# Loading image halves on two queues, constants behind the first image, weights prepared on GpSimd

## Chip, core and metric

The kernel runs on one core of a Trainium2 chip. The metric is the device time of one execution in microseconds. The engines are TensorE (PE; its weight loads are shown as PEld), VectorE (DVE), ScalarE (ACT), GpSimd (POOL) and SyncE (SP). SP and ACT each issue DMAs on a queue of their own.

## What is computed

The input `x` holds 2 batches ("images" below) of 56 channels of 128 by 128 numbers in float32. Two layers of a Fourier neural operator with attention are applied, each with a residual. `_conv_ref` is the same function for both, with its own weights:

```python
def fno_layer(x, w, b, sw, sb, norm=False, act=False):
    y = spectral_conv(x, w, b)          # rfft2, 32x16 modes times weights, irfft2
    if norm: y = inorm(y)
    y = y + skip1x1(x, sw, sb)
    return gelu(y) if act else y

def _conv_ref(x, ...):
    xa = x.reshape(B * K, 1, H, W)
    xn = inorm(xa, g1, b1)
    k, q, v = (fno_layer(xn, ...) for each of K, Q, V)      # 8 heads
    attn = softmax(einsum(q, k) / sqrt(H * W))              # over the 56 channels
    out = fno_layer(einsum(attn, v), Pw, Pb, Psw, Psb)
    att = inorm(out + xa, gan, ban)
    an = inorm(att, g2, b2)
    h = fno_layer(an, M0..., norm=True, act=True)
    h = fno_layer(h, M1..., norm=True, act=False)
    return inorm(h, gmo, bmo) + att

x = x + _conv_ref(_gn(x), layer 0 weights)    # _gn: group norm, 32 groups
x = x + _conv_ref(_gn(x), layer 1 weights)
```

## The kernel before

The Fourier transforms are matrix products with constant matrices. All constants lie in one array `const["all"]`; its first 128 columns are the identity, which the transposes need, and the rest (`group`, `fw`, `raw`, `same` and others) go into the tile `C` as well. `stage` takes the spectral weights of a layer, `smt` (tiles `sm0`, `sm1`) the small parameters of the two layers, each row spread over 128 partitions.

`X2` holds both images. An image is loaded as 8 DMAs of 448 KB (L209): for each pair `g` of row groups, one for each row half `c`, which goes to partitions 0 to 55 or 64 to 119. Two further DMAs (L214) fill the rows between.

The work of an image runs through stages:

- `turn` calls `turned` for 8 tiles. For each, PE transposes 16 pieces (L363) into a PSUM tile `pair`, of which there are three; ACT copies it to the plane `P` (L368); DVE takes two statistics (L373).
- `modes_chain` aggregates the statistics (L458), averages over groups on PE (L462), takes the square root on ACT (L466), scales the plane on DVE (L479) and ACT (L477), and transforms it (L483, L488, L386). POOL puts the factors into columns of `P` (L491, L493), PE turns them (L501), ACT copies the result to `gvr` (L503).
- `gram` sums the Gram matrix of the channels in 128 matmuls (L511), followed by `gram_chain`. `scale_x` multiplies `X2` by `gvr` on DVE (L550).
- `scores` (L597, L578), `softmax_chain` (L637 on), `values` (L620), `mix_chain`, `heads`, `norms_chain`, `gelu`, `h_chain` and `end` follow.

The weights go a way of their own. `prepare(layer, first, second)` combines weights and constants in elementwise operations (L255 to L302): those named `first` on one engine, those named `second` on another. Four wide ones (L270 to L273) come first, then two `product`s (L294 to L302), and `place` (L284 to L289) writes the result into `stage`. `relay` transposes that (L320, L324, L331) into `tc` (L335), and POOL widens `tc` into `WU` (`build`, L341), later into `WT` and `WM`. POOL also prepares parts of the scores (L572).

The two images are woven together by hand: the stages are generators that yield estimates of their cost, and `_woven` puts the second one's pieces between those of the first. A scheduler of the framework then orders the instructions of each engine by its own estimates, so an engine's final order isn't that of the source. It also puts in the semaphores. DMAs of both queues share eight of them in turn, so the issue of a DMA waits until the one eight places before it has landed.

Of the kernel before, what the change touches and what calls it, by code (L numbers as in the profile page):

```python
# [42 lines left out]
B, K, N = 2, 56, 128  # L43
# [11 lines left out]
N_CONST = sum(n for _, n in _PARTS.values())  # L55
# [73 lines left out]
N_SMALL = sum(n for _, n in _COLS.values())  # L129
# [11 lines left out]
def _woven(lead, *bulks):  # L141

    rest = chain(*bulks)
    for want in lead:
        while want > 0:
            cost = next(rest, None)
            if cost is None:
                break
            yield cost
            want -= cost  # L150
    yield from rest
# [9 lines left out]
def _run(units):  # L161
    for _ in units:
        pass
# [3 lines left out]
def fno_layers(ctx: ExitStack, tc: tile.TileContext, x, out, weights, small, const):  # L167
    nc = tc.nc
    V, S, G, T = nc.vector, nc.scalar, nc.gpsimd, nc.tensor
# [24 lines left out]
    Ct = cp.tile([N, N_CONST], F32, name="C")  # L194
# [1 line left out]
    ident = C["ident"]  # L196
    nc.scalar.dma_start(out=ident, in_=const["all"][:, :N])
    stage = cp.tile([N, 1632], F32, name="stage")
    nc.scalar.dma_start(out=stage[:, :1088], in_=weights[0].rearrange("p m r n t -> p (m r n t)"))
    smt = [cp.tile([N, N_SMALL], F32, name=f"sm{n}") for n in range(2)]  # L200
    for n in range(2):
        nc.scalar.dma_start(out=smt[n], in_=small[n : n + 1, :].to_broadcast([N, N_SMALL]))
    nc.scalar.dma_start(out=Ct[:, N:], in_=const["all"][:, N:N_CONST])
    X2 = xp.tile([N, B, 64, N], F32, name="X2")
    xin = x.rearrange("b k (g c r) w -> c b k g (r w)", c=2, r=8)
    for b in range(B):
        for g in range(0, 8, 2):
            for c in range(2):
                nc.sync.dma_start(  # L209
                    out=X2[64 * c : 64 * c + K, b, 8 * g : 8 * g + 16, :].rearrange("p (g r) w -> p g (r w)", r=8),  # L210
                    in_=xin[c, b, :, g : g + 2, :],
                )
    for b in range(B):
        nc.sync.dma_start(out=X2[K:64, b], in_=x[b, :8, :64, :])  # L214
    eps = cp.tile([N, 1], F32, name="eps")
# [138 lines left out]
    def turned(b, g, L, stats):  # L354
        p = pair()
        for s in range(2):
            for e in range(4):
                i = 8 * g + 4 * s + e
                if L == 0:
                    for c in range(2):  # L360
                        q = slice(64 * c, 64 * c + K)
                        o = K * (4 * s + e)
                        T.transpose(p[:, c, o : o + K], X2[q, b, i, :], ident[q, q], tile_position=(64 * c, 0))  # L363
                else:
                    T.transpose(p[:, s, N * e : N * e + 120], X2[:120, b, i, :], ident[:120, :120])  # L365
        dst = P[b][:, 896 * g : 896 * g + 896]
        if L == 0:
            S.copy(dst.rearrange("p (x c k) -> p c x k", x=8, c=2), p[:, :, :448].rearrange("p c (x k) -> p c x k", x=8))  # L368
        else:
            src = p.rearrange("p s (e c k) -> p (s e) c k", e=4, c=2)  # L370
            S.copy(dst.rearrange("p (x c k) -> p x c k", x=8, c=2), src[:, :, :, :K])  # L371
        for s in range(2):
            V.bn_stats(stats[:, 2 * g + s, :], dst[:, 448 * s : 448 * s + 448])  # L373

    def turn(b, stats):
        for g in range(8):
            turned(b, g, 0, stats)
            yield 0.9
# [74 lines left out]
    def new_stats(b):  # L453
        return little(f"stats{b}", [N, 16, 6])
# [478 lines left out]
    prs = [None, None]  # L933
    st = [[{}, {}], [{}, {}]]
    stats = [new_stats(b) for b in range(B)]
    par, d, cpt, tcs = prepare(0, V, G)
    prs[0] = par, d
    _run(turn(0, stats[0]))
    _run(_woven(
        chain(modes_chain(0, 0, stats[0], st[0][0]), relay(cpt, tcs, WT[:, 2048:3072], [(0, 16)])), turn(1, stats[1]),  # L940
    ))
# [1 line left out]
    for L in range(2):  # L943
# [13 lines left out]
        if L == 0:  # L957
            nc.sync.dma_start(out=stage[:, :1088], in_=weights[1].rearrange("p m r n t -> p (m r n t)"))
            par, d, cpt, tcs = prepare(1, G, G)
# [3 lines left out]
        stats = [new_stats(b) for b in range(B)] if L == 0 else [None, None]  # L963
# [61 lines left out]
```

## Time and profile before

| | us |
|---|---|
| runs of the kernel before | 555.65, 557.22, 564.92 |
| median | 557.22 |
| span of the profiled execution | 555.1 |
| PE busy in it | 457.0 (82%) |
| DVE busy | 337.0 (61%) |
| ACT busy | 190.2 (34%) |
| POOL busy | 184.3 (33%) |

The page gives the profiled execution's own time as its span, from the first to the last instruction; the fastest of the three runs is 0.55 us longer than it. The shares are averages over all stages. How an edit at the kernel's head acts is read from the head itself: from the chain of waits, which follows the last work back to what released it, from the timelines of the engines, and from tables of busy time in short stretches. A line such as `9.78 1.76 ACT L368 COPY P<-pair ... x2 [5.16 <-PE pair L363]` gives start, length, engine, line, operation, output and input, number of instructions, and in brackets the idle time ahead of it and what ended it. `SPq` and `ACTq` are the issue of DMAs.

### The profile page before, as it was taken

What the parts mean: (1) busy time and instruction counts of PE and PEld (TensorE: products, weight loads), DVE (VectorE), ACT (ScalarE), POOL (GpSimd) and SP (SyncE); (2) the same over time, 40 slices, a digit from 0 to 9 for tenths busy, and PEclk for the clock granted to TensorE, in tenths of its full rate; (3) what the DMA queues carried; (4) which work ended last, traced back from release to release, by engine and by line L of the source; (5) the groups of instructions that cost most, each with busy time, mean ns of one, the idle gap of its engine ahead of it and who ended that gap; (6) DMA issues with size and microseconds to landing.
All of it is one profiled execution on the core that took longest, in us unless ns stands there. A gap on an engine that the chain in (4) does not pass through costs nothing.

```text
span 555.1 us, 14768 instructions
## 1 busy us (share of the span) xinstructions
PE 457.0 (82%) x6630; PEld 316.3 (57%) x6630; DVE 337.0 (61%) x577; ACT 190.2 (34%) x238; POOL 184.3 (33%) x194
## 2 busy tenths in 40 slices
PE   2447889799999999798688859989999999979390
PEld 1423858669685555455563447768967556535250
DVE  0576478932717665869459995841253865677751
ACT  2344132063437556233103314124454656602000
POOL 2460424920271000065456871630000000035566
PEclk9999689899998999988667959989999999988586
DMA  8993000050000000056144541030000000017687
GB/s 202 213 197 58 4 2 2 5 145 4 2 3 1 1 2 1 1 166 198 53 132 133 168 127 14 2 105 4 2 2 2 1 1 2 2 33 225 191 230 285
DMA packets 16303, 40.58 MB, mean 73 GB/s; under 512 B 2528, under 2 KB 3296, under 8 KB 16224
## 3 DMA queue, kind: packets, MB, share of 16 engines
q1 hardware_dynamic: 15520, 38.25, 25.5%
q10 hardware_dynamic: 720, 1.39, 1.0%
q8 instruction: 52, 0.85, 0.6%
q14 instruction: 11, 0.09, 0.1%
HBM read 24.69 MB, written 14.68 MB: 71 GB/s over the span
## 4 chain that ended last, share of the span: by engine, by line
PE 43%; DVE 26%; DMA 8%; ACT 7%; POOL 7%; issue 5%; SPq 2%; POOLq 0%; ACTq 0%; DVEq 0%
PE pair L766 5%; DVE X L550 4%; PE pair L801 4%; PE pair L751 4%; PE pair L597 4%; DVE stats L373 4%; PE bank L511 3%; PE bank L578 3%; DMA C<-const_all 3%; DMA X<-store 3%; POOL P L918 3%; PE bank L690 3%; PE bank L789 2%; PE bank L483 2%; DMA xr<-store 2%
## 5 line engine op out<-in xcount | busy, mean ns | idle before, releaser
L821 DVE BATCH_NORM_STATS2 stats<-P 128x6 f32<-128x512 f32 x64 | 40.5, 681 | 19.3 <-ACT P L819 19.2
L916 DVE SCALAR_TENSOR_TENSOR P<-P,hs,pair 128x1024 f32<-128x1024 f32 x32 | 40.0, 1269 | 18.7 <-PE pair L766 18.7
L918 POOL TENSOR_TENSOR X<-P,xr 128x1024 f32<-128x1024 f32 x16 | 39.9, 2500 | 30.5 <-DVE P L916 16.5
L550 DVE TENSOR_TENSOR X<-X,gvr 120x1024 f32<-120x1024 f32 x32 | 49.3, 1568 | 0.0
L373 DVE BATCH_NORM_STATS2 stats<-P 128x6 f32<-128x448 f32 x64 | 35.7, 610 | 20.1 <-ACT P L368 10.1
L819 ACT ACTIVATE P<-pair 128x1024 f32<-128x1024 f32 x32 | 32.6, 1026 | 32.0 <-PE pair L766 31.3
L395 POOL MEMSET WT<- 128x256 f32 x4 | 1.3, 313 | 121.0 <-PE bank L789 88.3
L766 PE MATMUL pair<-X,Be 57*64 57x512 f32 x256 | 41.1, 742 | 0.0
L511 PEld LDWEIGHTS bank<-P 128*64 128x64 f32 (+1 forms) x1024 | 37.1, 158 | 2.9 <-issue 2.6
L511 PE MATMUL bank<-P 128*64 128x56 f32 (+1 forms) x1024 | 38.7, 244 | 0.0
L801 PEld LDWEIGHTS pair<-C,P 120*128 120x128 f32 x256 | 26.8, 143 | 20.9 <-issue 12.3
L766 PE MATMUL pair<-X,Bs 57*64 57x512 f32 x256 | 37.5, 627 | 0.0
L751 PE MATMUL pair<-C,WT 32*128 32x128 f32 x512 | 26.7, 319 | 11.3 <-DVE P L916 5.5
L597 PE MATMUL pair<-xf,WU 64*64 64x56 f32 x1024 | 35.9, 220 | 0.0
L597 PEld LDWEIGHTS pair<-xf,WU 64*64 64x64 f32 x1024 | 32.8, 134 | 5.0 <-issue 3.9
L751 PEld LDWEIGHTS pair<-C,WT 32*128 32x128 f32 x512 | 21.6, 214 | 23.6 <-issue 9.1
L801 PE MATMUL pair<-C,P 120*128 120x120 f32 x256 | 34.3, 277 | 0.4 <-ACT P L819 0.2
L341 POOL TENSOR_TENSOR WT<-tc,C 128x1024 f32<-128x1024 f32 x8 | 26.5, 3341 | 20.0 <-ACT tc L335 11.9
L802 ACT COPY WT<-pair 128x896 f32<-128x896 f32 x32 | 28.8, 906 | 12.5 <-PE pair L801 12.3
L363 PE MATMUL pair<-C,X 56*128 56x56 f32 x256 | 17.5, 292 | 18.6 <-DMA X<-x 12.8
L371 ACT COPY P<-pair 128x896 f32<-128x896 f32 x16 | 14.4, 902 | 46.7 <-PE pair L365 46.7
L365 PE MATMUL pair<-C,X 120*128 120x120 f32 x128 | 20.3, 313 | 10.2 <-POOL X L918 9.2
(249 smaller groups left out, 868.8 us busy)
## 6 DMA issues: line engine op xcount, KB each, us to landing
X<-x SPq DMA_DIRECT2D x16, 448.0 KB
xr<-x SPq DMA_DIRECT2D x32, 224.0 KB
store<-X SPq DMA_DIRECT2D x32, 224.0 KB
out<-P SPq DMA_DIRECT2D x32, 224.0 KB
xr<-store SPq DMA_DIRECT2D x16, 224.0 KB
X<-store SPq DMA_DIRECT2D x16, 224.0 KB
C<-const_all ACTq DMA_DIRECT2D x1, 621.0 KB
stage<-weights ACTq DMA_DIRECT2D x1, 544.0 KB
```

The source lines that it names most:

```text
L373: V.bn_stats(stats[:, 2 * g + s, :], dst[:, 448 * s : 448 * s + 448])
L511: T.matmul(p[u : u + m, :K], lhsT=P[b][:, K * i : K * i + m], rhs=plane[b][:, i, :], start=(i < 2), stop=(i == N - 1), tile_position=(0, u ...
L550: V.tensor_tensor(v, v, _bc(st["gvr"][:120], 1, 8), ALU.mult)
L597: T.matmul(p[64 * e : 64 * e + 64, k, K * a : K * a + K], lhsT=WUv[64 * e : 64 * e + 64, t + k, a, :], rhs=xv[64 * e : 64 * e + 64, t + k, ...
L751: T.matmul(both[j // 2][:, j % 2, N * e : N * e + N], lhsT=Z[32 * j : 32 * j + 32, o : o + N], rhs=C["gw"][32 * j : 32 * j + 32, :], start ...
L766: T.matmul(p[64 * c : 64 * c + 64, r, :], lhsT=Bs[q, :], rhs=X2[q, b, s : s + 4, :].rearrange("p e w -> p (e w)"), start=False, stop=True, ...
L801: T.transpose(p[:, r, N * e : N * e + 120], h3[:120, o : o + N], ident[:120, :120])
L802: S.copy(hT[v].rearrange("p r e c k -> p (r e) c k"), p.rearrange("p r (e c k) -> p (r e) c k", e=4, c=2)[:, :, :, :K],)
L819: S.activation(h3, both[v].rearrange("p r m -> p (r m)"), AF.Gelu)
L821: V.bn_stats(stats[:, 4 * A + 2 * v + r, :], h3[:, 512 * r : 512 * r + 512])
L916: V.scalar_tensor_tensor(h3, h3, st["hs"], both[v].rearrange("p r m -> p (r m)"), ALU.mult, ALU.add)
L918: G.tensor_tensor(dst, h3, back(n), ALU.add)
```

## The change

Each image's row half 0 is loaded by SP and row half 1 by ACT; before, SP loaded both. The identity is still the first DMA of ACT. The weights of layer 0 move from ACT's queue to SP's, behind image 0's loads; the rest of the constants stays on ACT but goes behind image 0's loads; the two small parameter rows go to the end of ACT's list. `prepare(0, ...)` is called behind image 0's `turn`, and with POOL as both engines, where DVE was the first and POOL the second.

```diff
     nc.scalar.dma_start(out=ident, in_=const["all"][:, :N])
     stage = cp.tile([N, 1632], F32, name="stage")
-    nc.scalar.dma_start(out=stage[:, :1088], in_=weights[0].rearrange("p m r n t -> p (m r n t)"))
     smt = [cp.tile([N, N_SMALL], F32, name=f"sm{n}") for n in range(2)]
-    for n in range(2):
-        nc.scalar.dma_start(out=smt[n], in_=small[n : n + 1, :].to_broadcast([N, N_SMALL]))
-    nc.scalar.dma_start(out=Ct[:, N:], in_=const["all"][:, N:N_CONST])
     X2 = xp.tile([N, B, 64, N], F32, name="X2")
     xin = x.rearrange("b k (g c r) w -> c b k g (r w)", c=2, r=8)
     for b in range(B):
         for g in range(0, 8, 2):
             for c in range(2):
-                nc.sync.dma_start(
+                (nc.sync, nc.scalar)[c].dma_start(
                     out=X2[64 * c : 64 * c + K, b, 8 * g : 8 * g + 16, :].rearrange("p (g r) w -> p g (r w)", r=8),
                     in_=xin[c, b, :, g : g + 2, :],
                 )
+        if b == 0:
+            nc.scalar.dma_start(out=Ct[:, N:], in_=const["all"][:, N:N_CONST])
+            nc.sync.dma_start(out=stage[:, :1088], in_=weights[0].rearrange("p m r n t -> p (m r n t)"))
+    for n in range(2):
+        nc.scalar.dma_start(out=smt[n], in_=small[n : n + 1, :].to_broadcast([N, N_SMALL]))
...
     stats = [new_stats(b) for b in range(B)]
-    par, d, cpt, tcs = prepare(0, V, G)
+    _run(turn(0, stats[0]))
+    par, d, cpt, tcs = prepare(0, G, G)
     prs[0] = par, d
-    _run(turn(0, stats[0]))
     _run(_woven(
         chain(modes_chain(0, 0, stats[0], st[0][0]), relay(cpt, tcs, WT[:, 2048:3072], [(0, 16)])), turn(1, stats[1]),
     ))
```

## The prediction

> **What bounds the kernel now.** I read the chain of waits first, over the first 150 us, then the timelines of ScalarE (ACT) and SyncE (SP), then the table of busy time in 2 us stretches. The chain's columns are start, length, engine and line.
>
> ```profile
> 2.85 17.36 DMA C<-const_all
> 20.31 0.73 DVE stage L270
> ...
> 26.61 7.92 DVE stats L373 x15
> 34.55 0.60 DVE mv L458
> 35.48 0.60 PE bank L462 x2
> 37.41 1.23 DVE P L479
> 38.77 3.17 PE bank L483 x10
> ...
> 62.85 4.46 PE bank L511 x86
> ```
>
> The constants take until 20.3 us to land. VectorE (DVE) then prepares the weights (L270 to L289) and only afterwards works off sixteen statistics of image 0, so the mode chain of image 0 starts at 34.6, its first matmul L483 at 38.8 and its Gram matrix L511 at 62.8. From there TensorE (PE) is near full: 48.8 of the 54.7 us up to the first softmax (L637 at 117.5) are PE busy.
>
> ```profile
> 3.34 1.28 ACT L368 ACT_TABLE_LOAD   x1 [3.34 <-issue]
> 9.78 1.76 ACT L368 COPY P<-pair 128x896 f32<-128x896 f32 x2 [5.16 <-PE pair L363]
> ```
>
> ACT is free of its five DMA issues at 3.3 us and empties the first transposed tile at 9.8. SP waits inside its own list of loads:
>
> ```profile
> SPq L209 <- DMA C<-const_all: 7.4, 2, 3.8
> SPq L209 <- DMA stage<-weights: 4.5, 1, 4.5
> SPq L209 <- DMA sm<-small: 4.1, 2, 2.2
> ```
>
> A load is not issued until an older transfer, of whatever queue, has landed: there are eight semaphores for DMAs, and the ninth DMA reuses the first's. The last table tells the rate (last two columns: DMA share, GB/s):
>
> ```profile
> 4.00:6.00 2.00, 0.14 (x1) 0.14 (x2) 0.00 (x0) 0.62 (x1) 0.00 (x0) 1.00 1.04 236
> 6.00:8.00 2.00, 0.33 (x2) 0.15 (x2) 0.00 (x0) 0.00 (x0) 0.00 (x0) 1.00 1.01 263
> 20.00:22.00 2.00, 0.90 (x16) 0.90 (x18) 1.65 (x3) 0.00 (x0) 0.00 (x0) 1.00 0.92 203
> ```
>
> With large rows on both queues the DMA engines move 236 to 263 GB/s, with SP's images alone about 200.
>
> **What the Trainium skill says.** "DMA: Bandwidth & Descriptors", Issuing engines are not separate DMA queues: both queues run on the same 16 engines, and a second issuer saves only issue time. The trace agrees on the sharing (weights, 544 KB, took until 11.1 us beside images) but the stretches above show some rate gained. The same page, Anatomy of one DMA — SWDGE (gpsimd) path: a semaphore wait is held by the issuing sequencer, not by the DMA engine; SP's waits above agree. "SBUF — State Buffer", Who interferes with whom: a GpSimd (POOL) operation and a DVE operation with two SBUF inputs lock each other out; here DVE L550 takes 1.22 us alone and three take 7.71 beside POOL's L341 at 91.7. "TensorE: Matmul & The Clock Gate", What's actually happening: a PE that has idled runs at half clock for some 3.4 us; here sixteen L331 take 3.75 us at 57.3 and 1.96 at 88.2.
>
> **The change, part by part** (line numbers of the kernel before; the order is that of the program as built.) Call X1 to X16 the sixteen 448 KB loads; odd ones go to SP, even ones to ACT.
>
> *1. What is gained.* DVE loses about 5.5 us of L270 to L289, and image 0 is loaded first. Landing at 234 KB/us (240 GB/s, my choice between 203 and 263): the identity and X1 by 5.8 as before, then 896 KB in 3.8 us per pair, X8 at 20.5 instead of 25.8. A chain that started then would save some 10 us. It doesn't start then.
>
> *2. ACT's queue, the main cost.* ACT now has ten DMA issues ahead of its first copy L368 instead of five, and seven carry a wait. In order: identity, X2, X4, X6, X8 (waits for the identity), constants (X2), X10 (X4), X12 (X6), X14 (X8), X16 (constants), sm0 (X10), sm1 (X11). So ACT can empty no tile until X10 and X11 have landed. After 20.5: weights beside X8 and constants (rows over 4 KB, which got about 40% of the bytes beside images before: 544 KB in 5.3 us of 263 GB/s) are done at 22.6 and 26.8, X9 at 25.7, X11 at 29.2, X10 at 30.6. Issuing sm0 and sm1 takes 1.0 (they took 1.18), the table load 1.28: first copy F = 33 instead of 9.8. At 262 GB/s F is 31, at 205 it is 37. Behind it wait PE (three pair buffers, so PE stops after three tiles), the statistics, everything. SP's own waits delay nothing: each is met before its queue runs dry.
>
> *3. From F to the first L483.* The built order puts L462 of image 0 after half of image 1's transposes and all L483 of image 0 after the rest. From F: DVE takes 16 statistics at 0.55, from F+0.9 to F+9.7; with two of image 1 and the aggregate 0.59, L462 runs at F+11.7. ACT copies (0.88 each) keep pace. Then tiles 13 to 16 cold at 1.2 us; ACT takes the square root only after copy 14 and a table load, F+17.3; DVE with statistics between reaches L479's end at F+20. Image 1 has landed by 42, no wait. First L483 at 53 instead of 38.8.
>
> *4. From L483 to L511.* It was 24 us with image 1's transposes between; now nothing is between, but PE idles on DVE: L483 cold 2.5, then the alternation of L488 (1.0) and L479 (1.2) and four more statistics of image 1 brings L386 to +11, L386 1.7, L498 and L503 0.9, one L550 1.2 (now ahead), L324 1.4, L331 cold 3.7: +20. L511 starts at 73 instead of 62.8: 10 us late.
>
> *5. GpSimd.* L270 to L289 on POOL, priced from the same lines of layer 1 (all on POOL): the three 544-wide at 1.35, the rest 10.8, small columns of both layers 5.8, L273 0.6, L572 four at 0.56. But sm0 stands behind X16 on ACT's queue: 1344 KB after X10 at 117 KB/us is 42.1, plus 2.4 as before, 44.5. After it 19.5 us remain, then L491 and L493 1.6: 65.6. L501 needs L493's output, and step 4 has L501 at F+32.7 = 65.7. So POOL is covered, by nothing to spare; each us more would be paid in full.
>
> *6. L511 to the softmax.* Equal PE work. Before, PE idled 5.9 us there. Now L483 of image 1 comes after the whole of L511 and waits for L479, behind four L550 that share the lock with L341: DVE ready at +14, PE there at +12. L386's chain of 7 to 9 us has only 6 of PE work beside it. Three L620 now precede the last L331 and wait 1.2 for POOL. Idle sum 8 to 9; against it the fixed chains could shorten by 2. I take +2; bounds -2 and +4. The tile order is the same on every engine after the softmax, bar POOL memsets and three early xr loads, both at nothing: POOL is idle from 132 to 149 and the DMA engines are idle from 46 us. All later work follows by data, so the shift stays.
>
> *Sum.* 10 + 2 = 12 on the span of 555.1: 567. The three runs' median is 2.1 above the span (the fastest is 0.55 above), so 569.
>
> **The rivals.**
> R1, POOL is the bound: if DVE's L479 and copies lock it out, or sm0's 128 short rows share worse, L493 ends 6 us later, L511 at 79: 575. For it: one L302 of layer 1 took 0.89 us where others take 0.44, and one L284 0.65 instead of 0.32. Against: from 26 to 34 us POOL ran such lines beside DVE 93% busy.
> R2, not slower by 2%, by one mechanism: two queues hold the 262 GB/s of 6 to 10 us. Then F is 31, L511 at 71, +8; with image 1 turned before L511, its chain fills PE and step 6 gives -2: +6, 563. It decides from about 245 GB/s with step 6 at zero. For it: the two stretches shown. Against: those rows were the weights', and stretches with constants show 238 to 246.
> R3, the change does what it says: ACT is not held, tiles leave as they land. Image 1's tiles are then done at 42, L511 at 62 if POOL too were early, 556; with POOL as in step 5 it is again 73. Against it: the waits stand in ACT's list ahead of the copies.
>
> **How the numbers follow.** Forecast 569: 0.40; R1 575: 0.17; R2 563: 0.38; R3 556: 0.05. Two per cent, about what a measurement of this kernel can tell from no change, is 546 to 568. Forecast and R1 make slower 0.57; R2 and R3 make the same 0.41, faster keeps 0.02. The range is 560 to 579: rate (2 to 4 us each way), step 6 (-4 to +2), R1 to its end.
>
> **What would show it.** Right: ACT's first copy L368 near 33 us, DVE idle before; constants landed by 27 and unused; L483 near 53, L511 near 73, softmax near 129; POOL's L255 waiting for sm till 44. Wrong: a copy of image 0 before 25 us, or L511 before 66. Rate right if X10 lands near 31.

## The result, and the profile after

The changed kernel takes 574.54 us (median of four runs, 573.5 to 578.59), the kernel before 557.33 beside it (555.65 to 564.92). The ratio is 1.0327, with a 95% interval of 1.0285 to 1.037: slower by 17 us. The profiled execution's span grew from 555.1 to 572.0. In what follows the ratios and intervals leave out executions in a slower state, the medians count them, and of e15_one_queue, whose profile is of a slower execution, only the head up to 43 us is read, where TensorE's clock was full. From L205 on, a line of the changed kernel has a number one higher than before: L368 is now L369, L511 is L512.

The chain of waits over the first 150 us (start, length, what) begins quite differently from before:

```profile
1.92 11.65 DMA X<-x
13.60 14.41 DMA X<-x
28.03 17.25 DMA sm<-small
...
65.57 0.41 POOL P L494 x2
66.03 0.81 PE bank L502 x2
...
73.42 3.60 PE bank L512 x64
```

Two image loads, the second issued when the first has landed, take until 28.0; only then are the small rows issued, and they need 17 us to land. The chain then goes through GpSimd to L494, which TensorE waits for, and so to L512 at 73.4 (62.8 before). ScalarE's timeline shows the queue that holds both:

```profile
1.17 4.96 ACTq L205 DMA_DIRECT2D X<-x  x4
10.34 0.36 ACTq L210 DMA_DIRECT2D C<-const_all  x1
13.60 11.58 ACTq L205 DMA_DIRECT2D X<-x  x4
28.03 0.84 ACTq L213 DMA_DIRECT2D sm<-small  x2
28.90 1.28 ACT L369 ACT_TABLE_LOAD   x1 [28.90 <-DMA X<-x]
30.20 4.14 ACT L369 COPY P<-pair 128x896 f32<-128x896 f32 x5
```

The first copy starts at 30.2, where it was at 9.8. The four issues at 13.60 take 11.58 us because each waits for an older transfer. GpSimd's and TensorE's timelines show the second hold:

```profile
45.35 0.21 POOL L256 TENSOR_TENSOR der<-sm 128x8 f32<-128x8 f32 x1 [15.67 <-DMA sm<-small]
```

```profile
66.03 0.80 PE L502 MATMUL bank<-C,P 128*128 128x128 f32 x2 [4.19 <-POOL P L494]
```

GpSimd waits 15.67 us for the small rows, and TensorE later 4.19 for GpSimd. The table of busy time in 2 us stretches shows that the two queues do move more than the 200 GB/s of SyncE's images alone:

```profile
10.00:12.00 2.00, 1.64 (x30) 1.64 (x31) 0.00 (x0) 0.00 (x0) 0.00 (x0) 1.00 0.94 290
18.00:20.00 2.00, 0.00 (x0) 0.00 (x0) 0.00 (x0) 0.00 (x0) 0.00 (x0) 1.00 0.91 273
```

In the second stretch all five engines stand at zero: the data arrive, and nobody works on them.

How far the changed kernel is behind at a few places (start in us):

| place | before | after | shift |
|---|---|---|---|
| first copy, L369 | 9.78 | 30.20 | 20.4 |
| first L484 | 38.77 | 48.87 | 10.1 |
| first L512 | 62.78 | 73.35 | 10.6 |
| softmax of image 0, L638 | 117.50 | 129.17 | 11.7 |
| softmax of image 1, L638 | 145.33 | 159.43 | 14.1 |
| first L917, end of layer 0 | 235.26 | 248.46 | 13.2 |
| eighth L917 | 261.89 | 278.31 | 16.4 |
| first L459 of layer 1 | 283.60 | 300.05 | 16.5 |
| span | 555.1 | 572.0 | 16.9 |

Two thirds of the loss are there at the first softmax. The rest comes later, mostly in two places: between the two softmaxes, and between the first and the eighth L917. The first of them is visible in VectorE's timeline, and GpSimd's for the same stretch:

```profile
143.85 0.62 DVE L707 SCALAR_TENSOR_TENSOR P<-P,D 128x448 f32<-128x448 f32 x1
144.51 3.12 DVE L708 TENSOR_TENSOR P<-P,D 128x448 f32<-128x448 f32 x1
```

```profile
143.88 0.68 POOL L710 COPY bm<-P 1x56 f32<-1x56 f32 x1 [3.15 <-DVE P L703]
144.52 1.33 POOL L271 TENSOR_TENSOR stage<-stage,C 128x544 f32<-128x544 f32 x1
145.82 1.33 POOL L272 TENSOR_TENSOR stage<-stage,C 128x544 f32<-128x544 f32 x1
```

L708 takes 3.12 us, in step with two wide products of layer 1's preparation. In the kernel before, it took 0.62, and GpSimd came to those products only 17 us after it. A memset that waits for TensorE stood ahead of them; in the changed kernel it comes behind them, at 163.3:

```profile
132.83 0.62 DVE L707 TENSOR_TENSOR P<-P,D 128x448 f32<-128x448 f32 x1
```

```profile
149.24 0.32 POOL L395 MEMSET WT<- 128x256 f32 x1 [16.37 <-PE pair L620]
149.51 1.35 POOL L270 TENSOR_TENSOR stage<-stage,C 128x544 f32<-128x544 f32 x1
```

### The profile page after: what moved, and what is told of

Same layout as the page of the kernel before. It is cut to its first block, busy times and chain, and to the rows that moved or that the text cites. A ratio compares the mean times of both kernels' runs of the same rounds, so it can differ in the third digit from the quotient of the medians.

```text
span 572.0 us, 14762 instructions
## 1 busy us (share of the span) xinstructions
PE 459.6 (80%) x6630; PEld 320.7 (56%) x6630; DVE 334.2 (58%) x558; ACT 189.4 (33%) x238; POOL 190.1 (33%) x213
## 4 chain that ended last, share of the span: by engine, by line
PE 42%; DVE 24%; DMA 12%; POOL 7%; ACT 7%; issue 5%; SPq 1%; POOLq 0%; ACTq 0%; DVEq 0%
PE pair L767 6%; DVE X L551 5%; DMA X<-x 5%; PE pair L752 4%; PE pair L802 4%; PE pair L598 4%; PE bank L579 3%; PE bank L691 3%; DMA sm<-small 3%; DMA X<-store 3%; PE bank L512 3%; DVE P L917 3%; PE bank L790 2%; PE bank L442 2%; PE bank L387 2%
## 5 line engine op out<-in xcount | busy, mean ns | idle before, releaser
L374 DVE BATCH_NORM_STATS2 stats<-P 128x6 f32<-128x448 f32 x64 | 35.9, 608 | 41.5 <-ACT P L369 30.0
L551 DVE TENSOR_TENSOR X<-X,gvr 120x1024 f32<-120x1024 f32 x32 | 51.7, 1642 | 4.5 <-ACT gvr L504 4.5
L917 DVE SCALAR_TENSOR_TENSOR P<-P,hs,pair 128x1024 f32<-128x1024 f32 x32 | 40.0, 1269 | 20.3 <-PE pair L767 20.3
L822 DVE BATCH_NORM_STATS2 stats<-P 128x6 f32<-128x512 f32 x64 | 40.5, 678 | 18.7 <-ACT P L820 18.6
L512 PE MATMUL bank<-P 128*64 128x56 f32 (+1 forms) x1024 | 39.0, 246 | 0.0
L512 PEld LDWEIGHTS bank<-P 128*64 128x64 f32 (+1 forms) x1024 | 37.7, 161 | 0.7 <-issue 0.5
L598 PEld LDWEIGHTS pair<-xf,WU 64*64 64x64 f32 x1024 | 34.4, 140 | 6.6 <-issue 5.7
L364 PE MATMUL pair<-C,X 56*128 56x56 f32 x256 | 15.0, 306 | 28.4 <-ACT P L369 16.4
L598 PE MATMUL pair<-xf,WU 64*64 64x56 f32 x1024 | 37.5, 227 | 0.0
L752 PE MATMUL pair<-C,WT 32*128 32x128 f32 x512 | 29.1, 334 | 9.3 <-DVE P L917 4.9
L752 PEld LDWEIGHTS pair<-C,WT 32*128 32x128 f32 x512 | 23.8, 226 | 21.4 <-DVE P L917 8.1
L364 PEld LDWEIGHTS pair<-C,X 56*128 56x128 f32 x256 | 14.0, 215 | 29.1 <-ACT P L369 16.6
```

The lines of the kernel that those rows point to most:

```text
L512: T.matmul(p[u : u + m, :K], lhsT=P[b][:, K * i : K * i + m], rhs=plane[b][:, i, :], start=(i < 2), stop=(i == N - 1), tile_position=(0, u ...
L551: V.tensor_tensor(v, v, _bc(st["gvr"][:120], 1, 8), ALU.mult)
L598: T.matmul(p[64 * e : 64 * e + 64, k, K * a : K * a + K], lhsT=WUv[64 * e : 64 * e + 64, t + k, a, :], rhs=xv[64 * e : 64 * e + 64, t + k, ...
L752: T.matmul(both[j // 2][:, j % 2, N * e : N * e + N], lhsT=Z[32 * j : 32 * j + 32, o : o + N], rhs=C["gw"][32 * j : 32 * j + 32, :], start ...
L822: V.bn_stats(stats[:, 4 * A + 2 * v + r, :], h3[:, 512 * r : 512 * r + 512])
L917: V.scalar_tensor_tensor(h3, h3, st["hs"], both[v].rearrange("p r m -> p (r m)"), ALU.mult, ALU.add)
```

## The experiments

The theory to be tested: ScalarE's queue holds its copies; the small rows at the end of that queue hold GpSimd, and TensorE waits for it; a changed order on GpSimd makes L708 slow. The main rivals: the preparation's move to GpSimd costs by itself, or two queues are bad by themselves. Here is what all runs gave (times in us; the ratio is to the kernel before, run beside it):

| run | first copy | first L484 | first L512 | softmax, image 0 | L708 | median | ratio (95%) |
|---|---|---|---|---|---|---|---|
| before | 9.78 | 38.77 | 62.78 | 117.50 | 0.62 | 557.33 | 1 |
| changed | 30.20 | 48.87 | 73.35 | 129.17 | 3.12 | 574.54 | 1.0327 (1.0285 to 1.037) |
| e1_small_early | 29.54 | 52.01 | 72.63 | 130.97 | 3.12 | 573.67 | 1.0273 (1.0182 to 1.0364) |
| e2_images_on_sync | 9.79 | 32.81 | 50.81 | 111.27 | 0.62 | 553.69 | 0.994 (0.9913 to 0.9968) |
| e3_prepare_only | 9.69 | 36.29 | 60.73 | 114.98 | 0.62 | 554.86 | 0.9961 (0.9937 to 0.9985) |
| e4_loads_only | 30.46 | 66.41 | 86.29 | 144.80 | 3.12 | 588.03 | 1.0535 (1.0447 to 1.0624) |
| e6_l710_behind | 29.89 | 48.68 | 72.09 | 130.55 | 0.62 | 570.0 | 1.0247 (1.0215 to 1.0279) |
| e9_small_on_sync | 22.77 | 43.12 | 64.07 | 119.59 | 1.83 | 559.37 | 1.004 (1.0011 to 1.007) |
| e5_first_image_split | 15.36 | 39.98 | 58.75 | 113.67 | 0.62 | 553.04 | 0.9946 (0.992 to 0.9972) |
| e7_gpsimd_queue | 15.99 | 37.95 | 63.54 | 121.20 | 3.12 | 563.92 | 1.0136 (1.0084 to 1.0189) |
| e12_pool_wait_only | 30.40 | 49.05 | 67.54 | 123.07 | 3.12 | 568.34 | 1.0206 (1.0156 to 1.0256) |
| e13_no_issue_behind | 26.86 | 50.58 | 70.35 | 125.77 | 3.12 | 567.55 | 1.02 (1.0142 to 1.0257) |
| e14_split_no_wait | 11.80 | 35.28 | 55.38 | 109.47 | 0.62 | 551.72 | 0.9917 (0.9896 to 0.9939) |
| e15_one_queue | - | - | - | - | - | 555.65 | 0.9972 (0.9941 to 1.0003) |

### One part of the change at a time

**e3_prepare_only**: the kernel before, with only the move of the preparation.

```diff
-    par, d, cpt, tcs = prepare(0, V, G)
-    prs[0] = par, d
     _run(turn(0, stats[0]))
+    par, d, cpt, tcs = prepare(0, G, G)
+    prs[0] = par, d
```

> The kernel before, with only the second part of the change: the turn of image 0 is written first, and GpSimd instead of VectorE does the four wide products of the preparation; all loads as before. Theory: GpSimd has everything by the time VectorE had it and is done with the preparation before 60 us, so nothing waits for it; VectorE's 5.5 us were beside the wait for the images: 557 us, within 2 us of before. Rival (the preparation on GpSimd is the cost): the TensorE waits at the product that L502 is in the changed kernel, 561 us or more. Rival (VectorE's relief is a gain): 552 us.

Measured: ratio 0.9961, a gain of some 2 us. VectorE's relief brings the first L484 from 38.77 to 36.29 and the softmax from 117.5 to 115.0; in the profiled execution all of this lead is lost again by the end of layer 0 (261.95 at the eighth L917, 261.89 before), so the trace doesn't show where the gain of the median lies. The rival that this part is the cost is out.

**e2_images_on_sync**: the changed kernel with `nc.sync` for all image halves; constants, weights and preparation stay as changed.

```diff
-                (nc.sync, nc.scalar)[c].dma_start(
+                nc.sync.dma_start(
```

> The changed kernel, with all image halves issued by SyncE again; constants, weights, small rows and the preparation on GpSimd stay as changed (the weights between the two images on SyncE). ScalarE then has four issues and none waits. Theory (ScalarE's queue holds the copies): first copy near 10 us, first L484 near 39, L512 near 63 to 65 although the images land at 200 GB/s again: 557 to 561 us. Rival (moving the four wide products to GpSimd costs by itself): GpSimd's preparation ends late, the TensorE waits at L502 and the time stays over 565 us. Rival (two-queue loading is worth something that is lost here): slower than the changed kernel, over 574 us.

Measured: 553.69 us, 0.994, below the theory's 557 to 561. With ScalarE free the first copy is at 9.79 again:

```profile
2.87 1.28 ACT L369 ACT_TABLE_LOAD   x1 [2.87 <-issue]
9.79 1.76 ACT L369 COPY P<-pair 128x896 f32<-128x896 f32 x2 [5.64 <-PE pair L364]
```

So all of the loss comes with the image halves that ScalarE issues and what they hold up; the rest of the change is a small gain. This run takes away the second queue and ScalarE's waits together; the runs with image 0 alone on two queues, below, part them.

**e4_loads_only**: the changed loads, with `prepare(0, V, G)` ahead of `turn` as before.

```diff
-    _run(turn(0, stats[0]))
-    par, d, cpt, tcs = prepare(0, G, G)
+    par, d, cpt, tcs = prepare(0, V, G)
     prs[0] = par, d
+    _run(turn(0, stats[0]))
```

> The changed kernel's loads (halves on two queues, constants and weights behind image 0, small rows last) with the preparation as before: four wide products on VectorE, written ahead of the turn. Theory: all of the loss comes with the loads. The small rows still land near 45, GpSimd still starts its part then and TensorE still waits for L494 some 4 us; VectorE's four products lie inside the time in which ScalarE is held: 574 us, 572 to 577. Rival (the preparation's move to GpSimd carries a good part): 565 us or less. What is not sure: VectorE now waits for the weights (about 15.5 us) ahead of the turn's statistics; if that shows, up to 577.

Measured: 588.03 us. The theory's 572 to 577 missed by 11, and for a reason that I had overlooked. VectorE's timeline:

```profile
27.35 0.23 DVE L296 TENSOR_TENSOR stage<-stage 128x64 f32<-128x64 f32 x1
46.04 0.42 DVE L274 TENSOR_TENSOR stage<-stage,sm 128x256 f32<-128x256 f32 x1 [18.46 <-DMA sm<-small]
```

The fourth wide product, L274, reads the small row. On VectorE, in order and ahead of the statistics, it holds VectorE until 46.0. So the two parts of the change are not additive: the move to GpSimd gains 2 us with the loads as before, and with the late small rows it saves 12 to 13 (13.5 by the medians, 588.03 against 574.54; 11.6 by the ratios).

### The small rows

**e1_small_early**: the two rows directly behind the identity on ScalarE.

```diff
     nc.scalar.dma_start(out=ident, in_=const["all"][:, :N])
...
+    for n in range(2):
+        nc.scalar.dma_start(out=smt[n], in_=small[n : n + 1, :].to_broadcast([N, N_SMALL]))
```

> The changed kernel, with the two small parameter rows issued directly behind the identity on ScalarE's queue instead of behind the images. ScalarE still issues eight half loads and the constants, most of them behind a semaphore wait, ahead of its first copy. Theory (two waits in a row): the first copy stays near 30 us and the first L484-type activation near 49, because ScalarE is still held; but GpSimd's preparation no longer waits for the small rows till 45.35, L494 is done well before the TensorE asks for it, the 4.2 us wait at L502 goes, and L512 starts near 69.5 instead of 73.4: about 570.5 us. Rival (ScalarE's queue alone; the GpSimd wait is beside the path): L512 still starts near 73, 574 us. Rival (everything came from the late small rows): L512 back near 63, 560 us or less.

Measured: 573.67, L512 at 72.63. L502 waits for GpSimd no more, but the first L484 is at 52.0, 3 us later than in the changed kernel, since the last halves of image 1 land at 45.0 by the chain of waits, and copies of image 1 stand ahead of image 0's square root on ScalarE. One wait is gone, another has come: this run didn't tell the theory from its rival.

**e12_pool_wait_only** does. The rows that are used come early on GpSimd's queue, and two unread loads keep ScalarE's waits.

```diff
+    for n in range(2):
+        nc.gpsimd.dma_start(out=smt[n], in_=small[n : n + 1, :].to_broadcast([N, N_SMALL]))
...
+    spare = [cp.tile([N, 100], F32, name=f"spare{n}") for n in range(2)]
     for n in range(2):
-        nc.scalar.dma_start(out=smt[n], in_=small[n : n + 1, :].to_broadcast([N, N_SMALL]))
+        nc.scalar.dma_start(out=spare[n], in_=small[n : n + 1, :100].to_broadcast([N, 100]))
```

> The changed kernel with the small rows that are used loaded early by GpSimd's queue; at the end of ScalarE's queue stand two loads of the same kind (100 of 126 columns) into tiles that nothing reads, so ScalarE is held by the same waits as in the changed kernel. Only GpSimd's wait for the small rows is taken away. Theory: first copy still near 30 us, first L484-type matmul near 49, but no wait for L494: TensorE's L502 near 62 instead of 66, L512 near 69.3 instead of 73.4; the VectorE lock of 3.12 us at L708 stays, since the order of GpSimd's later part stays: about 570.5 us. Rival (GpSimd's wait cost nothing, something else stands behind it at the same time): 574.5. Rival (small rows early in the transfers push the images back, as when ScalarE issued them first): first L484 at 51 to 52 and 573.

Measured: 568.34, ratio 1.0206 against 1.0327. First copy (30.40) and first L484 (49.05) are as in the changed kernel. TensorE's timeline (L505 and L515 are L502 and L512 here):

```profile
59.12 1.72 PE L390 MATMUL bank<-WT,C 128*64 128x448 f32 x8 [1.12 <-DVE WT L492]
60.78 0.49 PE L505 MATMUL bank<-C,P 128*128 128x128 f32 x2
...
67.54 3.67 PE L515 MATMUL bank<-P 128*64 128x56 f32 x64
```

L505 follows at once where it waited 4.19 us, and L515 starts 5.8 us earlier than L512 did. GpSimd's wait is real and costs about 6 us of the 17. That is more than the 4.19 of the wait itself: L390 also ran at full clock, 1.72 us for its eight matmuls, where the changed kernel's L387 took from 58.58 to 61.83 at half clock. So up to 1.5 of the 6 may belong to the clock.

**e13_no_issue_behind**: the same without the two unread loads.

> As the run with the unread loads, but without them: ScalarE's queue ends with the last image half, whose issue waits for the constants. It tells what the two last issues (0.84 us of issuing, and the wait for the tenth and eleventh image halves) cost on ScalarE. Theory: first copy about 3.5 us earlier than there (26.5 instead of 30), and the first L484 and L512 by up to as much, if the copies of image 1 that stand ahead of ScalarE's square root have landed by then: L512 at 66 to 69, 567 to 570 us. Rival (the images' landing, not the queue, is what the copies wait for by then): same as with the unread loads, 570.5. Rival (these two issues are the whole cost, as the run with small rows on SyncE suggests): under 562.

Measured: 567.55, the same as with them within the intervals. The first copy comes at 26.86, 3.5 us earlier as expected, but nothing follows from it. TensorE's timeline:

```profile
43.60 3.66 PE L364 MATMUL pair<-C,X 56*128 56x56 f32 x63 [5.01 <-DMA X<-x]
50.58 1.72 PE L484 MATMUL bank<-P,C 128*32 128x448 f32 x8 [3.33 <-DVE P L480]
```

The theory failed here and the first rival held: by then the wait is for rows of image 1, which land at 43.6. In ScalarE's order copies of image 1 stand ahead of image 0's square root, so image 0's chain waits for image 1's data.

**e9_small_on_sync**: the two rows on SyncE behind the weights.

```diff
             nc.sync.dma_start(out=stage[:, :1088], in_=weights[0].rearrange("p m r n t -> p (m r n t)"))
+            for n in range(2):
+                nc.sync.dma_start(out=smt[n], in_=small[n : n + 1, :].to_broadcast([N, N_SMALL]))
```

> The changed kernel with the small rows issued by SyncE directly behind the weights, no longer by ScalarE behind the images. ScalarE keeps its eight halves and the constants ahead of its first copy, and the order of the images stays. Theory (two waits in a row): small rows land by about 20 us, GpSimd is done before TensorE asks, no wait at L502; ScalarE's first copy still at 29 to 30, first L484 at 49 to 52, L512 at 69 to 72 instead of 73.4, 570 to 573 us. Rival (GpSimd's wait hides nothing else, its 4.2 us come off whole): 570. Rival (ScalarE's activation of image 0 stands behind copies of image 1, whose rows land later when the small rows go first, so the gain is lost there, as it was when ScalarE issued them first): 574.

Measured: 559.37, ratio 1.004; 570 to 573 was expected. Most of the loss is gone with two lines moved to another queue. TensorE doesn't wait for GpSimd's L494, ScalarE's first copy comes at 22.77, and, what counts more, TensorE gets the tile of image 1 that ScalarE needs ahead of its square root ten us earlier than in e13_no_issue_behind:

```profile
34.00 0.24 PE L364 MATMUL pair<-C,X 56*128 56x56 f32 x1 [3.09 <-DMA X<-x]
```

The two row loads hold SyncE's next image halves back to 17.2 us, and ScalarE's halves and the constants land earlier: its last issue, which waits for the constants, comes at 21.1, in the changed kernel at 24.9. Why the order of arrival changes by so much is not settled: no run here varied only that.

### The slow L708

**e6_l710_behind**: L710 must wait for L708; GpSimd's order then has the two wide products ahead of it.

```diff
+        if L == 0 and b == 0:
+            V.tensor_copy(bm, u[0:1, :K])
         G.tensor_copy(bm, Pm[0:1, :K])
```

> The changed kernel with one 1x56 copy added on VectorE behind L708 of image 0 in layer 0, into the tile that GpSimd's L710 then fills: L710 must wait for L708, and the program order that comes of it puts layer 1's first two wide products (L271, L272) ahead of it. Nothing of the loads is touched, so all up to the first softmax stays (L638 near 129.2). Theory (3.12 us of L708 are the lock with those products): L708 takes 0.62 again, image 1's softmax starts near 157 instead of 159.4, and the time falls by about 2.5 us to 572. Rival (the slack of the later stages swallows it, as they swallowed the preparation's lead when that was tried alone): L708 short, the end unchanged at 574.5. Rival (the lock isn't the cause): L708 stays at 3.1 us.

Measured: 570.0, ratio 1.0247. VectorE's and GpSimd's timelines:

```profile
145.88 0.62 DVE L708 TENSOR_TENSOR P<-P,D 128x448 f32<-128x448 f32 x1
```

```profile
143.36 1.34 POOL L272 TENSOR_TENSOR stage<-stage,C 128x544 f32<-128x544 f32 x1
146.85 0.22 POOL L712 COPY bm<-P 1x56 f32<-1x56 f32 x1 [2.15 <-DVE bm L711]
```

L708 is back at 0.62 (L712 is L710 here), and image 1's softmax starts at 158.4 although image 0's was 1.4 us later than in the changed kernel. e9_small_on_sync, whose order puts one of the two products ahead of L710 and one behind, has 1.83: half the loss for half the overlap. In both kernels L708 ends 0.5 us after the last product beside it. So it is shown that L708 waits for these products.

The shift against before now stays at 13.1 us from the softmax of image 0 to the first L917; in the changed kernel it went from 11.7 to 14.1 at the softmax of image 1 and was 13.2 at the first L917. So there the two kernels are level in the profiles, since this run was 1.4 us later at the first softmax: from L512 to there it had 15.0 us of half clock, the changed kernel 12.5. The whole gain, 4.5 us by the medians, is more than the 2.5 of L708, and what L708 alone is worth at the end is not isolated. A part of the gain lies at the end of layer 0: the shift at the seventh and eighth L917 is 13.1 and 14.7, in the changed kernel 15.1 and 16.4.

### Towards a better kernel

**e5_first_image_split**: the rows as in e1_small_early, and only image 0 on both queues.

```diff
-                (nc.sync, nc.scalar)[c].dma_start(
+                (nc.sync, nc.scalar if b == 0 else nc.sync)[c].dma_start(
```

> Small rows directly behind the identity on ScalarE; image 0 in halves on both queues, image 1 wholly on SyncE behind the weights; preparation as changed. ScalarE has eight issues, the last (constants) waits for a half of image 0. Theory (what holds the copies is the place of the waiting issues): ScalarE's first copy near 14.5 and not 30, image 0 complete near 21, and the first L484 between 29 and 36, depending on three copies of image 1 that stand ahead of ScalarE's square root: 551 to 557 us. Rival (two queues are bad by themselves, whichever loads they carry): over 565 us. Rival (image 0 earlier by 4 us counts in full): 550 us, faster than with all images on SyncE (553.7).

Measured: 553.04, ratio 0.9946. The first copy comes at 15.4 as expected, the first L484 only at 40.0 (three copies of image 1 ahead of the square root), and still it is as fast as e2_images_on_sync: two queues are not bad by themselves.

**e7_gpsimd_queue**: both images on SyncE and GpSimd, `(nc.sync, nc.gpsimd)[c]`, ScalarE free.

> Both images in halves on two queues as in the changed kernel, but SyncE's and GpSimd's; small rows behind the identity, and constants, on ScalarE, which has four issues and none that waits. Theory (ScalarE's held copies are the cost, two queues are not): first copy near 10 us, image 0 complete near 21, first L484 near 29, L512 under 62: 550 to 556 us. Rival (GpSimd's own issues hold its preparation or are slow): GpSimd's weights late, TensorE waits at L502, 560 us or more. Rival (two queues themselves, by contention for the same DMA engines, are the cost): image 0 no earlier than with SyncE alone, over 560 us.

Measured: 563.92, ratio 1.0136; 550 to 556 was expected. GpSimd issues its eight halves without a wait by 6.6 us, so image 1's compete with image 0's. A half that it issued at 3.5 landed at 28.3 (chain of waits: "3.47 24.78 DMA X<-x"), and image 0 was complete later than from SyncE alone: its last copies start at 29.43, in e2_images_on_sync at 24.95. That the order of the arrivals counts beside the rate is argued from these times, not shown by itself, since GpSimd's queue may differ in more than the order. Against the kernel before, the first L484 is not late (37.95); the loss shows at the softmax, with 3.7 us.

**e14_split_no_wait**: image 0 on both queues; constants, weights and image 1 on SyncE; small rows on GpSimd's queue. ScalarE has five issues, of which only the last waits, for the identity.

```diff
+    for n in range(2):
+        nc.gpsimd.dma_start(out=smt[n], in_=small[n : n + 1, :].to_broadcast([N, N_SMALL]))
...
-                (nc.sync, nc.scalar)[c].dma_start(
+                (nc.sync, nc.scalar if b == 0 else nc.sync)[c].dma_start(
...
-            nc.scalar.dma_start(out=Ct[:, N:], in_=const["all"][:, N:N_CONST])
+            nc.sync.dma_start(out=Ct[:, N:], in_=const["all"][:, N:N_CONST])
```

> A candidate for a better kernel: image 0 in halves on both queues, constants, weights and then image 1 on SyncE, small rows by GpSimd's queue. ScalarE has five issues, the last waits only for the identity (near 6 us). Theory (two queues give 250 to 300 GB/s and nothing is held by it): first copy near 9, image 0 complete by 18 to 20 instead of 24.5, constants by 22, first L484 at 26 to 29 (32.8 with the images on SyncE alone), then image 1 sets the pace: 548 to 552 us. Rival (the image's earlier arrival is swallowed by the wait for image 1 or later stages): 553 to 555, as the earlier two candidates.

Measured: 551.72, ratio 0.9917 (0.9896 to 0.9939), the best of all: 0.8% faster than the kernel before. ScalarE's timeline:

```profile
1.17 5.11 ACTq L207 DMA_DIRECT2D X<-x  x4
11.80 1.76 ACT L369 COPY P<-pair 128x896 f32<-128x896 f32 x2 [4.21 <-PE pair L364]
...
22.47 1.76 ACT L369 COPY P<-pair 128x896 f32<-128x896 f32 x2 [2.10 <-PE pair L364]
28.65 1.76 ACT L369 COPY P<-pair 128x896 f32<-128x896 f32 x2 [4.42 <-PE pair L364]
```

The last two copies of image 0 start at 22.5 (24.95 in e2_images_on_sync, 26.9 before). The next pair, at 28.65, is image 1's and stands ahead of the square root, so the first L484 comes at 35.3 and not at the 26 to 29 that were expected. The gain is there, but smaller than it could be.

**e15_one_queue** is its control: SyncE issues every half.

> The same as the candidate with the split first image, except that SyncE issues every image half: what the second queue for image 0 is worth with nothing held. Theory: image 0 complete near 21 to 23 (200 GB/s and nothing beside it), constants near 25, first L484 near 30, 551 to 555 us, 1 to 4 us more than with the split. Rival (the split is worth nothing): the same time as with it.

Measured: 555.65, ratio 0.9972 (0.9941 to 1.0003). By the ratios the split gains 3.1 us over it. That is not all shown to be the second queue: the last two copies of image 0 start only 1.2 us later here (23.71), no copy of image 1 stands ahead of the square root, and the first L484 comes at 32.78, earlier than in e14_split_no_wait. Against e2_images_on_sync, another order of loads from SyncE alone, e14_split_no_wait is ahead by 0.23% or 1.3 us, and there the intervals overlap. So the second queue, with the order of instructions that comes of it, is worth some 1 to 3 us.

## Why the prediction was right, and where its steps were off

569 was forecast, slower, with a range of 560 to 579; 574.5 was measured. The mechanism is as written in steps 2 and 5, ScalarE's queue and the late small rows. But several sizes were wrong and partly cancelled.

- **Step 2, first copy at 33.** It came at 30.2, and X10 had landed by 28.0 instead of 30.6. (The list given there is complete, but it has twelve issues, eight of them with a wait, not ten and seven.) The mis-sized term is the rate: 240 GB/s was chosen, and the twelve stretches of 2 us from 6 to 30 us show 249 to 301. R2 had named this rate. It didn't bring R2's 563, because of the next two points.
- **Step 3, first L484 at 53.** It came at 48.87: 18.7 us from the first copy, where 20 was taken.
- **Step 5, GpSimd done at 65.6.** L494 ended at 65.97, the small row landed near 45 instead of 44.5; this working held. "Covered by nothing to spare" did not, since TensorE was ready 3.9 us earlier than step 4 had it: 66.03 less the wait of 4.19 is 61.8, not 65.7. Removing the wait brought about 6 us. So L512 at 73 was met (73.35) by two errors that cancelled: the path through ScalarE was some 4 us faster, and then waited as long for GpSimd. R1's mechanism, GpSimd as the bound, decided this stage; R1's 79 for it did not come. The total next to R1's 575 is a coincidence.
- **Step 6, two us up to the softmax.** 1.1 were measured (73.35 to 129.17 against 62.78 to 117.50); the softmax came at 129.17, forecast 129.
- **"All later work follows by data, so the shift stays."** This is the step that failed: 11.7 became 16.9. The moved memsets were priced at nothing because GpSimd is idle there. Their price is not GpSimd's time. The memset that waits for TensorE had kept the wide products away from L708; with it behind them, L708 lost 2.5 us, as e6_l710_behind shows. Of these, 1.5 are left in the shift at the first L917 (13.2 against 11.7). I had quoted the lock between the two engines for L550 in the same text, and did not apply it to the moved instructions.
- **The remaining 3 us** appear at the end of layer 0, from 13.2 at the first L917 to 16.4 at the eighth. e4_loads_only, with the same loads, has 31.2 and 31.4 there, so the loads alone don't bring them. What goes with them is TensorE's clock. Summed over stretches of 0.25 us, the changed kernel has 17.1 us at half clock between these two places, the kernel before 6.8. Over the thirteen profiles without e15_one_queue, the length of this stage follows that sum: 25.7 and 25.8 us with 3.4 us of half clock, 26.6 to 26.9 with 6.8, 27.4 to 28.3 with 10.2, 28.5 with 13.7, 29.9 with 17.1. This is a relation between profiles, not an experiment. In layer 1 the same is seen in another place: e6_l710_behind lost 2.8 us against the changed kernel between L703 and L861, in the `gelu` stage, where its granted clock was 0.66 from 440 to 450 us with TensorE busy for 9.8 of the 10, and that of the changed kernel 1.00. What starts these stretches of half clock, and which would come back in another execution, one profile each can't tell; that part is open.
- **Step 1, the gain "doesn't start".** Right for the changed kernel. e14_split_no_wait shows what is left of the 10 us once nothing is held: 0.83% or 4.6 us against the kernel before, and of these e2_images_on_sync has 3.3 without the second queue.

## What to carry to other kernels

A DMA issued on a compute engine's queue costs its wait, not its issue time: twelve issues of some 0.4 us each held the first copy back by 20 us, because an issue waits for an older transfer and everything behind it waits with it. Put on such a queue only loads whose wait is over before the engine's first work, and place small loads by who needs them first, as these two rows of 63 KB each, which held two engines. And look at what a moved instruction had kept apart: even one that costs nothing can be the reason why two engines didn't collide.

## What the runs showed of the hardware

- Two issuing queues moved 249 to 301 GB/s in the stretches of 2 us from 6 to 30 us, where SyncE's images alone got about 200. In the last two of these stretches, with the constants landed and only image rows and the small rows under way, it was 287 and 295. The Trainium skill, "DMA: Bandwidth & Descriptors", section Issuing engines are not separate DMA queues, says that a second issuer saves only the sequencer's time of issuing. Here the measured rate differs and decides. In time it is worth little: the last copies of image 0 start 1.2 us earlier in e14_split_no_wait than in its control with one queue.
- TensorE's clock after a gap. In e1_small_early a gap of 3.84 us ahead of L541 left the next 36 matmuls at half clock (2.17 us):

```profile
115.25 0.64 PE L541 MATMUL bank<-vd,ones 56*128 56x56 f32 x2 [3.84 <-DVE vd L537]
115.82 2.17 PE L512 MATMUL bank<-P 128*64 128x56 f32 x36
```

  After 2.31 us in the changed kernel and 3.60 before, the same 36 ran at full clock (1.26 both times), but the clock fell to half 1.9 and 1.6 us after the gap's end. In e12_pool_wait_only a gap of 2.32 us there was followed by full clock up to 126 us, and in the changed kernel 2.56 us of idle time ahead of 41.33 by half clock from 41.5 on. So the gap's length alone doesn't decide it here. The Trainium skill, "TensorE: Matmul & The Clock Gate", section What's actually happening, gives an idle window of about 3.4 us that runs freely, whatever the kernel does. The lengths agree with such a window: the stretches at half clock last 3.4 us (before, from 104.2) or a multiple of it, 6.8 (e1_small_early, from 114.8), 10.2 and 13.7 (changed, from 41.5 and 65.4).
